# The state space model of the slice tokens, written anew: both directions on the two halves of the partitions, parameters loaded early, results kept transposed

## The chip, the cores and the metric

The kernel runs on one core of one Trainium2 chip. The metric is the device time of one execution in microseconds. A core has TensorE (PE in the profile; PEld are its weight loads), VectorE (DVE), ScalarE (ACT), GpSimd (POOL) and SyncE (SP). Each engine works through its own queue in order; DMA transfers run beside them. The granted clock is the share of its full clock that TensorE was given.

## The reference

A graph of 2708 nodes with 256 features goes through four layers, each an attention over the graph and a feed-forward block. The change lies in the feed-forward block of layer 0. There every node is softly assigned to 64 slice tokens in each of 8 heads, the tokens pass through a small state space model that runs both ways over the 64 tokens, and the result is handed back to the nodes:

```python
st = einsum('bhnc,bhng->bhgc', fx, sw) / (snorm + 1e-05)     # slice tokens: 64 tokens x 512
# _hydra(u = st):
zxbcdt = u @ in_w.T                 # gate z 512, x 512, B 64, C 64, dt 2*8
dt = softplus(concat(dt[..., :8], flip(dt[..., 8:])) + dt_bias)
xBC = silu(causal_conv(xBC, conv_w, 3 taps) + conv_b)
dA = exp(dt * -exp(A_log)); dBx = dt * B * x
h = h * dA_t + dBx_t; y_t = h . C_t                          # both directions
y = shift(y_fw) + shift(y_bw)
y = y + x * repeat(x @ fcD_w.T + Dp, 64)
yg = y * silu(z)
yg = yg * rsqrt(mean(yg**2) + 1e-05) * norm_w
ot = yg @ out_w.T
out = einsum('bhgc,bhng->bhnc', ot, sw) @ final_out_w.T      # back to the nodes
```

## The kernel before

All nodes lie in `X`, 22 tiles of 128 nodes by 256 features, float32. `cosine_gnn` is the graph attention of layer 0. `slice_ffn` follows. It allocates `swt` (the slice weights, transposed, of all nodes), `mix` and the output weights, then a pool `s_w` with the token sums `zs`, the weights `wfx`, `bfx`, `hyin` and `hyout` of the state space model, loaded through POOL's queue. The loop over the 22 node tiles computes logits, softmax and products; the sums of the tokens stay in four PSUM banks `zacc`. When the loop ends, DVE divides them into `zs` (lines 464 to 468), `hydra` runs, and a last loop of products (`po`, line 139 called from 477) adds `swt` times `mix` to `X`. Layer 1 begins from that `X`.

The order of each engine is chosen by a planner that places instructions as written, by priority, as soon as its model of the work says that they are ready; so work that is written earlier goes first where both are ready. `tc.issue_after` ties a block behind an instruction. `tc.manual_schedule(engines=...)` keeps the written order on the engines it names. In `slice_ffn` and `hydra` neither is used.

`hydra` turns the recurrence into matrices. For every head and direction, a 64x64 matrix of decays is the exponential of differences of cumulated sums, masked by a triangle, times B·C and the time step; both directions are shifted by one token and added into `km`. In order: transposes of `zs` into `zt` and `ztr` (L504, L508); the product with `wfx` and the bias, three products for each head (L139, L514), into `u`, 64 tokens on the partitions; four transposes of `u` to `ut` (L493); the gate `zg` with 512 columns at once and Silu (L523); the time step `dt`; the convolutions of x and of B and C (L543 to L554); x back to rows, `xr` (L561); softplus of `dt` by Exp and Ln (L567 to L581); the decays, two products for each head and direction (L615 to L619), each direction into its own bank of 64 partitions; on DVE and ACT min, Exp and three multiplications for each direction (L621 to L626); their sum in `km`; the product with `xr` (L650); the gate and the root mean square norm on rows (L651 to L660); transposes to `yt`; the product with `hyout` (32 passes, L139); and eight products with `outw` into `mix` (L671, L672). The PSUM pool `h_p` has three banks. Small parameters (`dtb`, `cw`, `cb`, `alog`, `fcd`, `dp`, `normw`) are loaded where they are used, through POOL's queue.

A float32 product appears in the profile as two passes of PE; a transpose as one.

Of the kernel before, what the change touches and what calls it, by code (L numbers as in the profile page):

```python
# [16 lines left out]
P = 128  # L17
# [375 lines left out]
def slice_ffn(net, wf, bf, early):  # L393
# [3 lines left out]
    with ExitStack() as ctx:  # L397
# [5 lines left out]
        with ExitStack() as c2:  # L403
            wp = c2.enter_context(tc.tile_pool(name="s_w", bufs=1))
            zs = wp.tile([P, 4, D + 1], F32, name="zs")
            wfx = net.load_weight(wp, a["w_fxT"], "wfx")
            bfx = wp.tile([1, HC], F32, name="bfx")
            nc.gpsimd.dma_start(bfx, a["b_fx"].partition_broadcast(1))
            hyin = net.load_weight(wp, a["hy_inT"], "hyin")
            hyout = net.load_weight(wp, a["hy_outT"], "hyout")  # L410
# [60 lines left out]
            hydra(net, wp, zs, wfx, bfx, hyin, hyout, outw, mix)  # L471
# [9 lines left out]
def hydra(net, wp, zs, wfx, bfx, hyin, hyout, outw, mix):  # L481


    nc, tc, a = net.nc, net.tc, net.a
    H, L, HC = 8, 64, 512
    ident = net.ident
    with tc.tile_pool(name="h_w", bufs=1) as w, tc.tile_pool(name="h_p", bufs=3, space=PSUM) as psum:

        def transposes(src, n, name):

            ps = psum.tile([P, n, L], F32, name="hp", tag="hp")
            for m in range(n):
                nc.tensor.transpose(ps[:, m, :], src[:, m * P : (m + 1) * P], ident[:L, :L])  # L493
            t = w.tile([P, n, L], F32, name=name)
            nc.scalar.copy(t, ps)
            return t


        zt = w.tile([P, 2, HC], F32, name="zt")
        ztr = w.tile([1, HC], F32, name="ztr")  # L500
        for c in range(2):
            ps = psum.tile([P, HC], F32, name="hp", tag="hp")
            for m in range(4):
                nc.tensor.transpose(ps[:, m * P : (m + 1) * P], zs[:, m, c * P : (c + 1) * P], ident)  # L504
            nc.scalar.copy(zt[:, c, :], ps)
        ps = psum.tile([1, HC], F32, name="hp", tag="hp")
        for m in range(4):
            nc.tensor.transpose(ps[:, m * P : (m + 1) * P], zs[:, m, D : D + 1], ident)  # L508
        nc.scalar.copy(ztr, ps)
        ps = psum.tile([L, HC], F32, name="hp", tag="hp")  # L510
        for h in range(H):
            hs = slice(h * L, (h + 1) * L)
            net.matmul_k(ps[:, hs], zt[:, :, hs], wfx[:, :, hs], last=False)
            nc.tensor.matmul(ps[:, hs], ztr[:, hs], bfx[:, hs], start=False, stop=True)  # L514
        u = w.tile([L, HC], F32, name="u")
        nc.scalar.copy(u, ps)
        ut = transposes(u, 4, "ut")


        pz = psum.tile([L, HC], F32, name="hp", tag="hp")  # L520
        net.matmul_k(pz, ut, hyin[:, :, 0:HC])
        zg = w.tile([L, HC], F32, name="zg")
        nc.scalar.activation(zg, pz, AF.Silu)  # L523
        pdt = psum.tile([L, 2, H], F32, name="hp", tag="hp")
        net.matmul_k(pdt.rearrange("p a h -> p (a h)"), ut, hyin[:, :, 1152:1168])
        dt = w.tile([L, 2, H], F32, name="dt")
        dtb = net.load_rows(w, a["dt_bias"], H, "dtb", L)
        nc.vector.tensor_tensor(dt, pdt, dtb.unsqueeze(1).to_broadcast([L, 2, H]), ALU.add)

        def conv(n, parts, offset, name):  # L530

            cw = w.tile([parts, n, 3], F32, name=f"cw{name}")
            nc.gpsimd.dma_start(
                cw, a["conv_w"][offset : offset + n * parts].rearrange("(n p) k -> p n k", p=parts)
            )
            cb = w.tile([parts, n], F32, name=f"cb{name}")
            nc.gpsimd.dma_start(cb, a["conv_b"][offset : offset + n * parts].rearrange("(n p) -> p n", p=parts))
            ps = psum.tile([parts, n, L], F32, name="hp", tag="hp")
            for m in range(n):
                o = HC + offset + m * parts  # L540
                net.matmul_k(ps[:, m, :], hyin[:, :, o : o + parts], ut)
            pad = w.tile([parts, n, L + 2], F32, name=f"pad{name}")
            nc.vector.memset(pad, 0.0)  # L543
            nc.scalar.copy(pad[:, :, 2:], ps)
            y = w.tile([parts, n, L], F32, name=f"y{name}")
            for m in range(n):
                nc.vector.tensor_scalar(
                    y[:, m, :], pad[:, m, 0:L], cw[:, m, 0:1], cb[:, m : m + 1], ALU.mult, ALU.add
                )
                for k in (1, 2):  # L550
                    nc.vector.scalar_tensor_tensor(
                        y[:, m, :], pad[:, m, k : k + L], cw[:, m, k : k + 1], y[:, m, :], ALU.mult, ALU.add
                    )
            nc.scalar.activation(y, y, AF.Silu)  # L554
            return y

        xt = conv(4, P, 0, "x")
        bc = conv(2, L, HC, "bc")
        ps = psum.tile([L, HC], F32, name="hp", tag="hp")
        for m in range(4):  # L560
            nc.tensor.transpose(ps[:, m * P : (m + 1) * P], xt[:, m, :], ident)  # L561
        xr = w.tile([L, HC], F32, name="xr")
        nc.scalar.copy(xr, ps)


        e = w.tile([L, 2, H], F32, name="e")
        nc.vector.scalar_tensor_tensor(e, dt, -1.0, dt, ALU.mult, ALU.max)  # L567
        nc.scalar.activation(e, e, AF.Exp, scale=-1.0)
        w1 = w.tile([L, 2, H], F32, name="w1")
        nc.vector.tensor_scalar(w1, e, 1.0, None, ALU.add)  # L570
        lg = w.tile([L, 2, H], F32, name="lg")
        nc.scalar.activation(lg, w1, AF.Ln)
        nc.vector.tensor_scalar(w1, w1, -1.0, None, ALU.add)
        same = w.tile([L, 2, H], F32, name="same")
        nc.vector.tensor_scalar(same, w1, 0.0, None, ALU.is_equal)
        nc.vector.tensor_tensor(w1, w1, same, ALU.add)
        nc.vector.reciprocal(w1, w1)
        nc.vector.tensor_tensor(lg, lg, w1, ALU.mult)
        nc.vector.tensor_tensor(lg, lg, same, ALU.add)
        nc.vector.tensor_tensor(lg, lg, e, ALU.mult)  # L580
        nc.vector.scalar_tensor_tensor(dt, dt, 0.0, lg, ALU.max, ALU.add)  # L581

        alog = net.load_rows(w, a["a_log"], H, "alog", L)
        nc.scalar.activation(alog, alog, AF.Exp)
        la = w.tile([L, 2, H], F32, name="la")
        nc.vector.scalar_tensor_tensor(
            la, dt, -1.0, alog.unsqueeze(1).to_broadcast([L, 2, H]), ALU.mult, ALU.mult
        )


        upper = w.tile([L, L], F32, name="upper")
        make_upper_triangular(nc, upper)
        strict = w.tile([L, L], F32, name="strict")
# [70 lines left out]
        for m in range(4):  # L664
            net.matmul_k(po[:, m, :], hyout[:, :, m * P : (m + 1) * P], yt)
# [1784 lines left out]
```

## Time and profile before

| | |
|---|---|
| median of 3 runs | 2646.69 us (2646.11 to 2649.6) |
| profiled execution | 2647.78 us |
| its span | 2646.0 us |
| mean granted clock | 0.962 |
| PE busy in the span | 2446.7 us (92%) |
| DVE, ACT, POOL busy | 1476.4 (56%), 1060.2 (40%), 329.2 us (12%) |
| slice loop, 410 to 500 us | PE 96% busy |
| state space model, 502.6 to 562.7 us | PE 74% busy, clock 0.63 |
| `po` loop, 562.7 to about 603 us | PE 97% busy or more |

Stages are given in microseconds from the start of the span. Busy shares of PE are of pipelined instructions whose ends are modelled: durations of single instructions overlap, and the distance from one start to the next is what a stream costs. The span is shorter than the execution by what lies around it, 1.8 us.

### The profile page before, as it was taken

Reading aid. Unit: us, or ns where it says so; the run is one execution under the profiler, and the core shown is the slowest. Engines: PE = TensorE matmul, PEld = TensorE weight load, DVE = VectorE, ACT = ScalarE, POOL = GpSimd, SP = SyncE. Lnnn points to the kernel's source line nnn. Section 1 sums busy time; section 2 is a strip of 40 time slices with the busy share of each in tenths; the row PEclk is TensorE's granted clock in tenths of the full one; section 3 lists DMA queues with packets and bytes.
Section 4 is the critical chain, followed back from the end, with each engine's and each line's share of the span. In section 5 each row is a group of like instructions: output and inputs, shape, how many; then the busy total and the mean of one; then the engine's idle time right before and its main releaser. Section 6 shows DMA issues by size and latency. Waiting matters only on the chain. (4 is left out here: it accounts for less than half of the span.)

```text
span 2646.0 us, 32568 instructions
## 1 busy us (share of the span) xinstructions
PE 2446.7 (92%) x11676; PEld 1581.2 (60%) x11676; DVE 1476.4 (56%) x3258; ACT 1060.2 (40%) x1714; POOL 329.2 (12%) x445
## 2 busy tenths in 40 slices
PE   5999999887999998979799989999899999969998
PEld 4666765574333334468578854444357777747887
DVE  7754348544788886333545457787653222264556
ACT  3444443313787772321434323334422222234454
POOL 1000002100000001134130011222231111110002
PEclk9999999978999999989899999999989999989999
DMA  8899520000000002774310010000231111050001
GB/s 289 281 299 320 172 86 31 3 6 1 1 1 1 1 1 82 170 193 144 91 62 1 1 38 9 19 17 17 101 128 50 33 33 33 22 203 7 1 1 43
DMA packets 106875, 197.70 MB, mean 75 GB/s; under 512 B 8846, under 2 KB 63736, under 8 KB 103876
## 3 DMA queue, kind: packets, MB, share of 16 engines
q1 hardware_dynamic: 88010, 146.82, 17.8%
q0 software_dynamic: 14896, 43.89, 5.1%
q10 hardware_dynamic: 3806, 4.85, 0.6%
q8 instruction: 98, 1.61, 0.3%
q14 instruction: 65, 0.53, 0.1%
HBM read 135.82 MB, written 59.71 MB: 74 GB/s over the span
## 5 line engine op out<-in xcount | busy, mean ns | idle before, releaser
L701 DVE SCALAR_TENSOR_TENSOR e<-e,mask 128x768 f32<-128x768 f32 (+3 forms) x352 | 417.0, 1215 | 241.9 <-ACT e L700 239.1
L700 ACT ACTIVATE e<-big_p,minus_one,ratio 128x768 f32<-128x768 f32 (+3 forms) x352 | 418.6, 1226 | 285.2 <-PE acc L1371 196.8
L1371 PE MATMUL acc<-V,e 128*128 128x257 f32 x1848 | 405.3, 382 | 5.7 <-DVE e L701 5.6
L1371 PEld LDWEIGHTS acc<-V,e 128*128 128x128 f32 x1848 | 352.7, 191 | 58.6 <-issue 7.0
L2125 PE MATMUL h<-w,ft 128*128 (+1 forms) x752 | 233.9, 452 | 1.3 <-DVE yl L1955 1.3
L307 PE MATMUL acc<-F,e 128*128 128x257 f32 (+1 forms) x924 | 212.5, 383 | 3.7 <-DVE e L303 3.4
L836 PE MATMUL acc<-e,V 128*64 128x512 f32 (+1 forms) x1056 | 209.1, 548 | 2.2 <-DVE e L701 2.2
L307 PEld LDWEIGHTS acc<-F,e 128*128 128x128 f32 (+1 forms) x924 | 171.6, 189 | 56.6 <-DVE e L303 29.2
L2142 DVE TENSOR_TENSOR hh<-hh,h 128x682 f32<-128x682 f32 x47 | 40.7, 865 | 243.7 <-PE h L2125 243.7
L2125 PEld LDWEIGHTS h<-w,ft 128*128 128x128 f32 x752 | 135.8, 191 | 57.2 <-issue 1.8
L836 PEld LDWEIGHTS acc<-e,V 128*64 128x64 f32 x1056 | 73.7, 138 | 151.3 <-issue 146.1
L1922 ACT ACTIVATE e<-sc 128x1024 f32<-128x1024 f32 (+4 forms) x131 | 107.1, 863 | 139.2 <-PE sc L1913 116.6
L303 DVE TENSOR_TENSOR e<-e,mask 128x512 f32<-128x512 f32 (+2 forms) x132 | 80.5, 621 | 141.3 <-ACT e L296 139.6
L1944 DVE TENSOR_TENSOR sum<-sum,e 128x1024 f32<-128x1024 f32 (+4 forms) x131 | 135.2, 1032 | 40.1 <-ACT e L1922 19.6
L296 ACT ACTIVATE e<-score 128x512 f32<-128x512 f32 (+2 forms) x132 | 69.4, 544 | 170.4 <-PE score L294 145.1
L2157 PE MATMUL po<-w,ht 114*128 (+1 forms) x564 | 131.5, 383 | 0.9 <-DVE ht L2150 0.9
L1913 PE MATMUL sc<-qt,kt 64*128 64x512 f32 (+5 forms) x568 | 123.9, 555 | 1.4 <-ACT sum L1922 0.9
L2157 PEld LDWEIGHTS po<-w,ht 114*128 114x128 f32 x564 | 107.6, 192 | 23.0 <-DVE ht L2150 8.2
L847 PE MATMUL den<-e,low 128*3 128x512 f32 (+1 forms) x1056 | 117.7, 542 | 0.0
L294 PE MATMUL score<-QK 128*128 128x512 f32 (+2 forms) x264 | 112.0, 553 | 3.4 <-ACT e L296 3.0
L1938 PE MATMUL po<-e,V 128*64 128x512 f32 (+5 forms) x524 | 111.2, 543 | 1.7 <-DVE e L1928 1.7
L2151 ACT COPY ht<-pt 114x256 f32<-114x256 f32 x47 | 17.5, 372 | 201.0 <-DVE ht L2150 201.0
(652 smaller groups left out, 3408.4 us busy)
## 6 DMA issues: line engine op xcount, KB each, us to landing
row<-in_adj SPq DMA_DIRECT2D x21, 1354.0 KB
raw<-in_adjT SPq DMA_DIRECT2D x35, 768.0 KB
hs<-zero SPq DMA_DIRECT2D x8, 2838.0 KB
hidden<-hr SPq DMA_DIRECT2D x32, 256.0 KB
wd<-in_f_wd SPq DMA_DIRECT2D x8, 1024.0 KB
kept<-mask SPq DMA_DIRECT2D x21, 338.5 KB
mask<-kept SPq DMA_DIRECT2D x21, 338.5 KB
w<-in_d_w1T SPq DMA_DIRECT2D x8, 682.0 KB
```

The costliest lines, as they stand in the source:

```text
L294: nc.tensor.matmul(ps[:r, :iw], QK[:, 0, span(j)], QK[:, 1, i0 : i0 + iw], start=True, stop=True)
L307: ended = nc.tensor.matmul(acc[k], e[:r, k * P : (k + 1) * P], F[:r, j, :], start=j == 0, stop=j == NT - 1)
L700: nc.scalar.activation(v, big_p[:, i], AF.Relu, bias=net.minus_one, scale=ratio)
L701: return nc.vector.scalar_tensor_tensor(v, v, 1.0, net.mask[:, j, i], ALU.add, ALU.mult)
L836: nc.tensor.matmul(acc[n][half, :iw], V[:, j, h, :], e[n][:, k, :iw], start=j == 0, stop=j == NT - 1)
L847: nc.tensor.matmul(den[g : g + Q, :iw], low[:, j, h, Q - 1 - q : 2 * Q - 1 - q], e[n][:, k, :iw], start=False, stop=j == NT - 1 and q == Q ...
L1371: nc.tensor.matmul(acc[k][:ri], e[:, k * P : k * P + ri], V[:, j, :], start=j == 0, stop=j == NT - 1)
L1913: nc.tensor.matmul(by_pairs(ps[:r, g], m, iw)[:, :, o:], kt[b, span(j)], qt[b, :, o:iw], start=True, stop=True)
L1938: nc.tensor.matmul(by_pairs(outs[n, p][b], m, iw)[:, :, o:], V[:r, j, g, :], by_pairs(e[:r, g], m, iw)[:, :, o:], start=j == 0, stop=j == ...
L1944: nc.vector.tensor_tensor(total, total, by_heads(e[:r], m, iw)[:, :, :, o:], ALU.add)
L2125: last = nc.tensor.matmul(halves[s, n][:, q, :HALF], fts[s][:, c, :], weights.w13[n][:, es[s], c, q * HALF : (q + 1) * HALF], start=c == 0 ...
L2157: last = nc.tensor.matmul(po, ht[:KP, k, :], w2[:KP, es[s], k, :], start=k == 0, stop=k == KC - 1)
```

## The change

`hydra` becomes a class. Its constructor stands where the weights were loaded, ahead of the slice loop, and now also loads all small parameters, takes the exponential of `a_log`, multiplies the rows of `hyout` by `norm_w`, clears the padding and `km`, and makes the triangles and a selector `pick`. `run` stands where `hydra` was called. It uses `manual_schedule` for PE, ACT and DVE, with seven PSUM banks.

- The product with `wfx` writes its result transposed, even heads on partitions 0 to 63 and odd heads on 64 to 127, so `u` and its transposes go.
- The forward direction lives on partitions 0 to 63 and the backward one on 64 to 127. Time step, softplus, min, Exp and the masks are done once for both. The half of the decays that doesn't depend on the row is one product of 512 columns for each direction. The sum over the directions is left to the product with `xr`, which holds x twice.
- The gate is computed transposed: 32 passes of 64 columns with full weight loads for 8 of 512 columns.
- y stays transposed: `yt` and its transposes go. The norm's factor is applied at the end, when `mix` is copied, on ACT and DVE in turn. The sum of squares is a product with ones.

```diff
-            wfx = net.load_weight(wp, a["w_fxT"], "wfx")
...
+            layer = Hydra(net, wp)
...
-            hydra(net, wp, zs, wfx, bfx, hyin, hyout, outw, mix)
+            layer.run(zs, outw, mix)
...
+    def __init__(self, net, pool):
+        self.wfx = net.load_weight(pool, a["w_fxT"], "wfx")
...
+        self.hyin = net.load_weight(pool, a["hy_inT"], "hyin")
+        self.hyout = net.load_weight(pool, a["hy_outT"], "hyout")
+        self.fcd = net.load_weight(pool, a["fcdT"], "fcd")
+        self.dtb = net.load_rows(pool, a["dt_bias"], H, "dtb")
+        self.alog = net.load_rows(pool, a["a_log"], H, "alog")
+        nc.scalar.activation(self.alog, self.alog, AF.Exp)
...
+        nc.gpsimd.dma_start(normw, a["norm_w"].rearrange("(c p) -> p c", p=P))
+        for c in range(4):
+            nc.vector.tensor_scalar(self.hyout[:, c, :], self.hyout[:, c, :], normw[:, c : c + 1], None, ALU.mult)
+        self.taps = {}
+        for name, n, parts, offset in (("bc", 2, L, HC), ("x", 4, P, 0)):
...
+            nc.gpsimd.memset(pad, 0.0)
+            self.taps[name] = n, parts, offset, cw, cb, pad
...
+        make_upper_triangular(nc, self.seen[low])
+        make_lower_triangular(nc, self.seen[high])
+        make_upper_triangular(nc, self.rise[low])
+        make_upper_triangular(nc, self.rise[high], val=-1.0, diag=False)
+        nc.vector.tensor_scalar(self.fall, self.rise, -1.0, None, ALU.mult)
+        self.pick = pool.tile([H, H, L], F32, name="pick")
+        nc.vector.tensor_copy(self.pick, net.ident[:H, :H].unsqueeze(2).to_broadcast([H, H, L]))
+        self.km = pool.tile([P, H, L], F32, name="km")
+        nc.gpsimd.memset(self.km, 0.0)
...
+            nc.vector.tensor_copy(ztr, pr)
+            nc.scalar.copy(zt[:, 0, :], pz[0])
+            nc.vector.tensor_copy(zt[:, 1, :], pz[1])
...
+                here = ps[halves[h % 2], h // 2, :]
+                nc.tensor.matmul(here, self.bfx[:, hs], ztr[:, hs], start=True, stop=False, skip_group_check=True)
+                for c in range(2):
+                    nc.tensor.matmul(
+                        here, self.wfx[:, c, hs], zt[:, c, hs], start=False, stop=c == 1, skip_group_check=True
+                    )
+            ut = w.tile([P, 4, L], F32, name="ut")
+            nc.scalar.copy(ut, ps)
...
+            front("bc")
+            front("x")
...
+            bc = convolved("bc")
+            nc.scalar.activation(bc, bc, AF.Silu)
+            pk = bank([P, H, L])
+            for b in halves:
+                nc.tensor.matmul(
+                    pk[b], self.fall[b], la[b].unsqueeze(2).to_broadcast([L, H, L]),
+                    start=True, stop=False, skip_group_check=True,
+                )
+            for h in range(H):
+                for b in halves:
+                    nc.tensor.matmul(
+                        pk[b, h, :], la[b, h : h + 1].to_broadcast([L, L]), self.rise[b],
+                        start=False, stop=True, skip_group_check=True,
+                    )
+            xt = convolved("x")
+            nc.scalar.activation(xt, xt, AF.Silu)
...
+            nc.vector.tensor_scalar(k, pk, 0.0, None, ALU.min)
+            nc.vector.tensor_tensor(gm, pg, self.seen, ALU.mult)
+            nc.scalar.activation(k, k, AF.Exp)
+            px = bank([P, HC])
+            for m in range(4):
+                for b in halves:
+                    nc.tensor.matmul(
+                        px[b, m * P : (m + 1) * P], xt[:, m, :], ident, start=True, stop=True, skip_group_check=True
+                    )
...
+            for m in range(4):
+                net.matmul_k(pz[:, m, :], hyin[:, :, m * P : (m + 1) * P], ut)
+            zg = w.tile([P, 4, L], F32, name="zg")
+            nc.scalar.activation(zg, pz, AF.Silu)
...
+                    pd[:, m, :], self.pick[:, 2 * m : 2 * m + 2, :].rearrange("h k l -> h (k l)"), fc,
...
+                    py[halves[h % 2], h // 2, :], xr[:, hs], km[:, h, :], start=True, stop=True, skip_group_check=True
...
+            nc.vector.tensor_tensor(y, py, through, ALU.add)
+            nc.vector.tensor_tensor(y, y, zg, ALU.mult)
+            sq = w.tile([P, 4, L], F32, name="sq")
+            nc.scalar.activation(sq, y, AF.Square)
+            po = bank([P, 4, L])
+            for m in range(4):
+                net.matmul_k(po[:, m, :], self.hyout[:, :, m * P : (m + 1) * P], y)
...
+            nc.scalar.activation(rs, ss, AF.Sqrt, bias=net.ln_eps, scale=1.0 / HC)
+            nc.vector.reciprocal(rs, rs)
+            ot = w.tile([P, 4, L], F32, name="ot")
+            nc.scalar.copy(ot, po)
+            for m in range(4):
+                pm = bank([P, D])
+                for b in halves:
+                    nc.tensor.matmul(pm[b], ot[b, m, :], outw[b, m, :], start=True, stop=True, skip_group_check=True)
+                if m % 2:
+                    nc.scalar.activation(mix[:, m, :], pm, AF.Copy, scale=rs)
                 else:
+                    nc.vector.tensor_scalar(mix[:, m, :], pm, rs, None, ALU.mult)
```

## The prediction

> **What bounds the kernel now.** I read the page, then a table of stages, then the groups by shape and the timeline of the state space model. The page's chain that ended last covers only the final 36 us, so this stage has to be read on its own. Stages first (stretch, length, busy PE, weight loads, DVE, ACT and POOL with counts, granted clock, DMA share, GB/s):
>
> ```profile
> 402.00:410.00 8.00, 5.64 (x20) 2.59 (x19) 7.56 (x18) 4.75 (x7) 3.29 (x5) 1.00 0.28 82
> 410.00:500.50 90.50, 86.72 (x363) 57.36 (x361) 75.35 (x138) 30.60 (x60) 19.18 (x38) 1.00 0.00 1
> 502.60:562.70 60.10, 44.32 (x275) 33.59 (x274) 19.85 (x65) 18.36 (x33) 8.26 (x18) 0.63 0.05 9
> ```
>
> The slice loop (410 to 500) is PE's, 96% busy. While it starts (402 to 410), DVE is the full engine. The state space model is 60.1 us of one chain: PE 74%, DVE 33%, ACT 31%, at a mean clock of 0.63. The same columns inside it:
>
> ```profile
> 506.00:508.00 2.00, 1.87 (x17) 1.40 (x18) 0.00 (x0) 0.37 (x1) 2.00 (x4) 1.00 0.21 5
> 508.00:510.00 2.00, 2.00 (x13) 1.53 (x14) 0.38 (x2) 0.00 (x0) 2.00 (x9) 0.50 0.10 2
> 516.00:518.00 2.00, 2.00 (x3) 0.47 (x3) 0.00 (x0) 0.12 (x1) 0.00 (x0) 0.50 0.00 0
> 518.00:520.00 2.00, 2.00 (x5) 0.55 (x4) 0.00 (x0) 0.00 (x0) 0.00 (x0) 0.94 0.00 0
> 528.00:530.00 2.00, 1.00 (x5) 0.55 (x5) 1.76 (x11) 1.14 (x3) 0.00 (x0) 0.62 0.00 0
> 552.00:554.00 2.00, 2.00 (x12) 2.00 (x11) 0.00 (x0) 0.00 (x0) 0.00 (x0) 0.50 0.00 0
> ```
>
> PE falls to half clock at 508, returns at 518 after the 512-column products of the gate (L139, hp<-hyin,ut), falls again at 528 and stays low to 566. At 552 PE is busy without a gap and still at 0.50: the 64-column stream with full weight loads doesn't lift the clock. Shapes (count, busy us, mean ns):
>
> ```profile
> L139 PE MATMUL hp<-yt,hyout 128*128 128x64 f32 x32 | 7.1, 423 | 0.5 <-ACT yt L495 0.5
> L139 PE MATMUL hp<-ut,hyin 128*128 128x64 f32 x32 | 3.8, 276 | 0.0
> L836 PE MATMUL acc<-e,V 128*64 128x512 f32 (+1 forms) x1056 | 209.1, 548 | 2.2 <-DVE e L701 2.2
> L294 PE MATMUL score<-QK 128*128 128x512 f32 (+2 forms) x264 | 112.0, 553 | 3.4 <-ACT e L296 3.0
> ```
>
> The first two are one shape at half and at full clock: 0.22 and 0.12 us each. The last two are 512 columns at full clock: 0.20 us each in L836, whose products alternate between two column halves of the array, 0.42 in L294, which has the whole array. So neighbouring halves overlap here. Last, the timeline at half clock (start, length):
>
> ```profile
> 530.44 0.44 PE L615 MATMUL hp<-upper,la 64*64 64x64 f32 x2
> ...
> 537.43 1.02 PE L139 MATMUL hp<-fcd,yx 128*64 128x8 f32 x8
> ...
> 562.73 7.50 PE L139 MATMUL po<-mix,swt 128*128 128x256 f32 x26 [0.46 <-ACT mix L672]
> ```
>
> 64 decay products, all in one quadrant, fill 530.44 to 537.43: 0.11 us each. The result is needed at 562.73.
>
> **The Trainium skill.** "TensorE: Matmul & The Clock Gate", Part 1, says PE runs at half clock by default, is released after a busy window of about 3.4 us, and loses it after an idle one. The trace agrees in the levels and, in 516 to 520, in the length; it adds that small products don't count as busy. Part 3 there says products in different row or column groups run at once; L836 agrees at 0.20 against 0.42. "TensorEngine Tiling (Array Packing)", Key Properties, says a change of tiling mode drains PE. "ScalarE: Activation LUTs", What ACT_TABLE_LOAD costs, has 1283 ns; the six loads here take 1.28 us each.
>
> **The change, in order**, on the clock of before and at half clock after 508.
>
> *Start.* The transposes end at 504.9 either way. The bias product now comes first and waits for `ztr`, which DVE copies ahead of the second half of `zt` (0.68 each, as L621's PSUM read): first head complete near 506.5, before 506.6. The products are the same 48, ending at 513.05. Gain 0.
>
> *Transposed results.* `u`, its four transposes and their copy go: 513.09 to 514.87 becomes one copy of 0.37 and a 0.06 hand-over, so PE resumes at 513.48. Gain 1.4.
>
> *PE from there*, counting two passes per product, 0.22 for a full load, 0.11 for a half load, and half of that where neighbours take different halves or quadrants: time step 16 at 0.055, 0.9; B and C 16 at 0.11, 1.8; x 32 at 0.22, 7.1; decays 4 of 512 columns at 0.85 (eight times 64 columns) in two quadrants, 1.7, and 32 at 0.055, 1.8 (before 7.0 for all); B times C 0.3; x as rows, 16 of 128 columns at 0.22 in two halves, 1.8; gate 32 at 0.22, 7.1; fcD 0.9; wait for `fc` 0.5; its spread over the heads, 8 at 0.22, 1.8; y 0.9; wait for DVE's two passes (0.3 to drain, twice 0.42 as 128x256, hand-overs) 1.2; output 32 at 0.22, 7.1; squares 0.9; root, `ot` copy and hand-overs 1.05; mix, 16 of 256 columns at 0.43 in two quadrants, 3.4 (seven banks, so no wait for a slot, where before three had PE wait for the copies); last copy 0.75. Sum 41.0: 513.5 + 41.0 = 554.5, against 562.73. Gain 8.2.
>
> *What lies under it.* Softplus and its table loads (513.5 to 519) hide under the x products, which end at 523.3. Then pad copy 0.6, twelve convolution passes 2.45 (as L547 and L551) and Silu 0.4 give x at 526.8, while the decays and B times C keep PE until 527.1: cover 0.3; without it each us is paid. The Silu of B and C stands behind the pad copy on ACT, which waits for PE at 523.3, plus 1.28 of table: ready 525.3, before PE asks at 526.8. The min, Exp and three kernel products on DVE (about 4 us) hide under the gate's 7.1. The Sqrt waits for the squares and `ot` is queued behind it, with all of mix behind that: that is the 0.9 and 0.3 in the sum. The deferred norm removes four 64x512 passes of DVE (0.68 to 0.74) and yt, about 4.7 us of the old chain, inside the 8.2. Memsets and triangles moved to POOL lay under PE before: 0.
>
> *Early loads.* Nine DMA issues of 0.53 to 0.78 move from 505 to 513 to about 390 to 396 on POOL, behind hyin and hyout; in front of outw and outb, which wait for space until 403 anyway. POOL's column of ones for the slice tokens shifts by some 9 us; its first use is after 405. New there: Exp of a_log on ACT (0.2) and four scalings of hyout on DVE, 128x512 each. Bounds 0.41 (the 64x504 copy) to 0.68; I take 0.55, so 2.2. They need the hyout and norm weights, whose queue drains near 401, so they fall where DVE is 95% busy and PE waits: paid in full. Cost 2.4.
>
> *Clock.* The decays and x rows are now dense over two quadrants or halves for 5.6 us, as dense as the gate products of before that lifted the clock. Released by about 528.7, the gate takes 3.8 instead of 7.1, and fcD, spread and y half: 5.1; a window that ends off that point costs about 1, so 4. Against it, the small steps before the output (fcD to y, about 4 us, mostly waiting) may drop it again. I take gained, then dropped.
>
> Sum: −8.2 − 4.0 + 2.4 = −9.8. The profiled execution took 2647.78 (span 2646.0, 1.8 around it), so 2638.0; the median of the runs is 1.1 lower, so 2636.9.
>
> **Rivals**, in the runs' median.
> A. Clock low throughout, as it was in 528 to 566: −8.2 + 2.4, 2640.9. For it: even a busy 552 to 554 stayed low. Against: dense pairs are another load.
> B. The forecast: 2636.9.
> C. The clock holds through the output: 3.3 there, 2.1 in squares and mix, and 1.6 in the first 3.3 us of po, which ran at half (562.7 to 566): 2629.9.
> D. Halves don't overlap for such short products: 0.9 (time step), 3.5 (decays), 1.8, 0.9, 0.9 come back, 8.0 in all, and no release: −0.2 + 2.4, 2648.9. L836 speaks against it, but with 512 columns.
> E. Slower: the scheduler places Exp of a_log or the first scaling where it thinks the load has landed, ahead of the graph stage's last exponentials or X updates. The load is behind 3.9 MB and tiny-element transfers; waited for from 392 to 406, ACT or DVE stands for up to 14 us, and with it the masks, X and the slice loop. −8.2 + 2.4 + 14 gives 2654.9. Past 5.8 us of stall there is no gain left under A. Before shows POOL waiting 3.4 us for outb in this place, so such waits happen.
>
> **Chances.** A 0.24, B 0.34, C 0.14, D 0.15, E 0.13. 0.2% is 5.3 us, about what a measurement of this kernel can tell from no change: faster means below 2641.4. A lies at the edge (0.18 of it faster), B and C are faster (0.47): 0.65. Same: the rest of A, D, short stalls: 0.23. Slower: long stalls and D with a stall: 0.12. The range for 8 in 10 runs from 2627 (C and a scaling that costs nothing) to 2649 (D); B's own is 2632 to 2640.
>
> **What would show it.** Right: PE resumes one copy after the last bias product; pairs of decay products start within 0.02 us; a granted clock of 1.00 in the gate products; the stage near 48 us; 2 to 3 us more between 400 and 410. Wrong: 64x64 products still 0.11 apart; clock 0.50 from 508 to the end; PE waiting for the Silu of x; a gap of several us on ACT or DVE that a load ended before 406; the graph stage after 604 put in another order.

## The result

The changed kernel takes 2641.03 us in the median of 17 runs (2630.93 to 2648.87), the kernel before 2648.32 us beside it (17 runs, 2643.68 to 2653.82). The ratio is 0.9973, with a 95% interval from 0.9962 to 0.9985: between 4.0 and 10.1 us faster, 7.3 by the medians. The profiled execution took 2634.70 us (span 2633.0, mean clock 0.966). It is one of the faster ones, so its 13 us against the profiled execution of before are not all the change's.

Stages of the changed kernel, the columns as in the prediction (stretch, length, busy PE, weight loads, DVE, ACT, POOL with counts, granted clock, DMA share, GB/s):

```profile
402.00:410.00 8.00, 5.02 (x9) 2.09 (x10) 3.38 (x11) 2.42 (x5) 6.76 (x18) 0.57 0.35 83
416.00:507.00 91.00, 87.56 (x371) 58.26 (x370) 76.28 (x142) 30.63 (x61) 17.54 (x36) 1.00 0.00 1
509.20:557.10 47.90, 42.20 (x310) 35.05 (x309) 15.19 (x53) 12.41 (x21) 1.81 (x3) 0.61 0.04 8
```

The slice loop itself is as it was. The state space model is 47.9 us long where it was 60.1, and PE is busy for 88% of it. But from 402 to 410, where DVE had 7.56 us of work, it now has 3.38, PE has about half as many instructions as before (9 for 20), and the granted clock, 1.00 before, is 0.57.

Inside the state space model, the timeline of PE of the changed kernel (start, length, instruction, idle time before it and what ended it):

```profile
533.04 1.97 PE L616 MATMUL hp<-la,fall 64*64 64x512 f32 x4
534.81 1.56 PE L622 MATMUL hp<-rise,la 64*64 64x64 f32 x30
...
537.63 3.79 PE L139 MATMUL hp<-ut,hyin 128*128 128x64 f32 x32
...
545.14 6.12 PE L139 MATMUL hp<-yh,hyout 128*128 128x64 f32 x32 [1.10 <-issue]
...
557.09 1.13 PE L139 MATMUL po<-mix,swt 128*128 128x256 f32 x4 [0.57 <-ACT mix L701]
```

The decays that filled 7 us are done in some 3.3 us (L616 and L622). The gate's 32 passes take 3.79 us, which is full clock; the output's 32 passes, of the same shape, 6.12, which is nearly all half clock. The clock records put the rise at 535.9 and the next fall at 546.2. `po` starts at full clock at once; before, its first 3.3 us ran at half.

**The ledger.** I paired each instruction that both programs hold and took the difference of its two start times. It is −0.5 us up to 380 us (nothing has changed there), +6.7 from 420 us to the end of the loop, −5.7 at the first `po`, −7.3 once `po` has caught up the half clock of before, and −13.0 at the end. So 7.2 us are lost between 380 and 410, 12.2 are gained from the last product of the loop to the first `po` (60.02 against 47.80 us), 1.6 in `po`, and 5.7 after that. In that last part both run the same instructions; what differs is the clock: the half-clock stretches after 570 us add up to 146.8 us before and 133.1 in the changed kernel's profile, and 13.7 us at half clock are worth up to 6.8. The first three terms make −6.6, close to the medians' −7.3. The prediction had −9.8.

### The profile page after: what moved, and what is told of

It reads as the page before. It is cut to its first block, busy times and chain, and to the rows that moved or that the text cites. A ratio compares the mean times of both kernels' runs of the same rounds, so it can differ in the third digit from the quotient of the medians.

```text
span 2633.0 us, 32640 instructions
## 1 busy us (share of the span) xinstructions
PE 2437.3 (93%) x11710; PEld 1579.9 (60%) x11710; DVE 1475.6 (56%) x3254; ACT 1053.4 (40%) x1703; POOL 330.9 (13%) x450
```

## The experiments

Each was compared with the kernel before on the same chip, in interleaved runs. The "jump" below is the shift of the loop (taken at 420 us) less the shift at 380 us. The "stage" runs from the end of the last product of the slice loop to the start of the first `po`: 60.0 us before, 47.8 in the changed kernel.

### Where do 7 us go before the loop?

Some names first: in the loop `f` is a tile of normalised nodes, `ft` its transpose, `pl` its logits and `sw` its slice weights; `e` and `g` are scores and sums of the graph layer ahead of the loop. `rise` and `fall` are triangles for the decays: POOL makes `rise`, and DVE makes `fall` from it.

The prediction had put 2.4 us there, for operations moved into a busy place. My first theory was just this with a larger size: the early operations hold up tile 0 in the queues. The rival was memory: the early tiles take 6.9 KB per partition (1 KB being 1000 bytes), which moves everything allocated after them. Two kernels undo the order, one makes the memory shift alone.

First, everything late:

```diff
+    def prepare(self):      # small loads, exponential, scaling, fills, triangles, pick
...
                 for t in range(NT + 2):
...
+                    if t == 6:
+                        layer.prepare()
```

> The changed kernel with everything of the state space model's constructor except the four weight loads (w_fx, b_fx, hy_in, hy_out) put into a method that the slice loop calls at tile 6: small loads, exponential of a_log, scaling of hy_out, zero fills, triangles, pick. The tiles keep their places in memory; the computation is the same. In the changed kernel the slice loop runs 6.7 us later than in the kernel before (the shift arises between 380 and 410 us). Theory O (the shift comes from these operations standing ahead of tile 0's work in the queues of DVE, ScalarE and GpSimd): the shift of the loop falls to under 1 us and the kernel to about 2635, some 6 us under the changed kernel. Rival M (the shift comes from the 6.7 KB per partition that the early tiles take, which moves the loop's work tiles onto memory that is freed later): the shift stays at 6 to 7 us and the time near 2641.

Measured: 2644.11 us, ratio 0.9982 (0.9972 to 0.9991). Jump 9.2 us.

Second, the loads stay and only the operations move:

> As the kernel above, but the nine small loads stay in the constructor and only the computing operations (exponential, scaling, fills, triangles, pick) move to tile 6 of the slice loop; the computation is the same. If the operations on DVE and ScalarE (pick ahead of tile 0's normalisation, scaling and exponential ahead of tile 0's logits) make the shift, it falls to under 1.5 us, time near 2635 to 2636. If GpSimd's queue of loads makes it (loads of 0.5 to 0.8 us of issue each, behind which the ones column of the first f tiles waits until 410 us), the shift stays at 5 to 7 us, time near 2641. Rival M also says 6 to 7 us.

Measured: 2642.25 us, ratio 0.9973 (0.9964 to 0.9983). Jump 8.4 us.

Third, the kernel before with a tile that nothing uses:

```diff
             hyout = net.load_weight(wp, a["hy_outT"], "hyout")
+            wp.tile([P, 1250], F32, name="unused")
```

> The kernel before with one unused tile of 5 KB per partition beside its weights (6.7 KB don't fit), so that the work tiles of the slice loop move in memory as in the changed kernel; nothing else differs and the computation is the same. Theory O: no shift in the slice loop, ratio 1.000 within 0.1 per cent. Rival M: the loop runs 5 to 7 us later, ratio 1.002 to 1.003.

Measured: 2655.27 us, ratio 1.0023 (1.0014 to 1.0032): slower than before, with no work more: the built program has the same instructions and two more waits. Jump 5.8 us.

The theory missed in all three runs, and the rival's cause is real. The first two runs don't acquit the operations, though. Written at tile 6, the scalings of `hyout` were still placed between 403.8 and 408.2 us, since the planner takes work that is ready; and in both, `fall` kept DVE waiting for POOL's triangle, for 3.36 and 2.50 us, after which PE stood for 2.89 and 2.68 us.

The profiles say how memory does it. In the kernel before, DVE has a pause at 399.5 us while it waits for the graph layer's last sums, and three tiles are normalised in it (timeline of DVE, kernel before):

```profile
399.50 1.03 DVE L124 TENSOR_SCALAR f<-X,mv,rstd 128x256 f32<-128x256 f32 x3
```

In the changed kernel the same pause stays empty, and the first `f` is written after the last work on the graph layer's tiles (timeline of DVE, changed kernel):

```profile
400.55 0.14 DVE L321 COPY den<-g 20x1 f32<-20x1 f32 x1 [1.44 <-ACT g L319]
...
401.68 0.47 DVE L327 SCALAR_TENSOR_TENSOR X<-F,s,X 20x256 f32<-20x256 f32 x1
...
402.53 0.39 DVE L124 TENSOR_SCALAR f<-X,mv,rstd 128x256 f32<-128x256 f32 x1
```

The unused tile does the same to the kernel before. Its timeline of PE:

```profile
403.64 0.66 PE L132 MATMUL tp<-ident,f 128*128 128x128 f32 x2 [2.96 <-DVE mv L161]
404.82 3.78 PE L139 MATMUL pl<-wf,ft 128*128 128x512 f32 x4 [0.52 <-ACT ft L429]
```

PE is starved for some 3 us, and then the logits take 3.78 us where they take 1.98 at full clock: the records show half clock for 6.8 us from 402.6. As the programs lay out their tiles, the pool of `f`, `ft` and `sw` ended 1.3 KB below the pool with the graph layer's last `e` and `g`. In the changed kernel it reaches 5.6 KB into that pool, in the third experiment 3.7 KB. Only the `sw` tiles and a few small ones lie in the shared part, but the pool waits as a whole. In the instruction streams of the changed kernel and of the third experiment, the first `f` carries a wait for TensorE's last product of the graph layer (L91) and stands behind DVE's last work on `X`; in the kernel before it has no such wait and stands 45 instructions earlier. And the third experiment shows that the unused tile alone does it.

So the next kernel brings the pools apart again, and leaves all early operations but the fills and the copy into `pick` early:

```diff
-        self.pick = pool.tile([H, H, L], F32, name="pick")
-        self.km = pool.tile([P, H, L], F32, name="km")
...
+            km = w.tile([P, H, L], F32, name="km")           # in run; the pads too
+            pick = w.tile([H, H, L], F32, name="pick")
```

> The changed kernel with the tiles pick and km and the padded convolution inputs (5.7 KB per partition) allocated, zeroed and filled in the state space model's own pool at its start in place of the constructor, so that the early tiles take 1.2 KB and the slice loop's work tiles end 0.1 KB below the first graph layer's work tiles (scores e and g), as they do in the kernel before (there 1.3 KB below). All loads, the exponential, the scaling, the fills of the triangles stay early; the computation is the same. Theory M (the loop's first tile waits because its pool reaches into memory of the graph layer's last scores): the jump of about 7 us between 380 and 410 us falls to 0 to 2.4 us (the scaling and the exponential that the prediction counted), and the time to 2634 to 2637. Rival O (the operations ahead in the queues): the jump stays at 5 to 7 us and the time near 2641.

Measured: 2637.26 us, ratio 0.9967 (0.9954 to 0.9980). Jump 5.9 us, so theory M, taken alone, missed as well. `f` of tile 0 is indeed early again (389 us), but PE now stops one tile later, for `f` of tile 1 (timeline of PE):

```profile
408.98 0.66 PE L132 MATMUL tp<-ident,f 128*128 128x128 f32 x2 [4.67 <-DVE f L124]
```

and DVE has four scalings of `hyout` in front of that `f` (timeline of DVE, same kernel):

```profile
406.60 1.84 DVE L499 TENSOR_SCALAR hyout<-hyout,normw 128x512 f32<-128x512 f32 x4
408.36 0.15 DVE L167 RECIPROCAL rstd<-sd 128x2 f32<-128x2 f32 x1
408.44 0.71 DVE L124 TENSOR_SCALAR f<-X,mv,rstd 128x256 f32<-128x256 f32 x2
```

With the operations early, the planner sets this `f` behind the softmax of tile 0 and the scalings; in the kernel before it went into the pause at 399.5. The scalings are only 1.84 of the 4.67 us, and ACT's wait of 1.56 us for `a_log` (404.36) comes before them too; what else holds this `f` was not separated.

Each cure alone leaves the other cause in place. Both together:

> The changed kernel with both cures of the early part together: the small loads and the early operations put to tile 6 of the slice loop, and pick, km and the padded inputs in the state space model's own pool, so that the loop's work tiles stay clear of the last graph layer's. The computation is the same. Each cure alone left the jump between 380 and 410 us at 6 to 9 us. Theory B (two causes, each of which alone holds the loop back: memory for the tiles' first writes, and the queues of DVE, ScalarE and GpSimd for the first tiles' further work; each is enough to starve TensorE once, which then runs at half clock for 6.8 us): with both gone the jump falls under 1.5 us, no half-clock stretch lies between 395 and 425 us, and the time is near 2635. Rival (something else, such as the weight loads or the planner's other order): the jump stays at 5 us or more and the time near 2640.

Measured: 2630.75 us, ratio 0.9938 (0.9925 to 0.9952). Jump 2.2 us. Its stage from 402 to 410 has the full clock again:

```profile
402.00:410.00 8.00, 4.60 (x14) 1.92 (x12) 7.67 (x15) 5.33 (x9) 6.45 (x10) 1.00 0.31 83
```

So there were two causes, each enough to starve PE for 3 to 5 us and to bring a half-clock stretch on top, and they overlapped instead of adding. One is the memory. The other is the early operations together with their small loads, which the last kernel moved at once and no run separates. The traces point to one operation that the prediction priced at nothing. In the changed kernel DVE stands until POOL has finished a triangle (timeline of DVE, changed kernel):

```profile
409.95 0.25 DVE L519 TENSOR_SCALAR fall<-rise 128x64 f32<-128x64 f32 x1 [4.28 <-POOL rise masks.py:66]
```

POOL makes its triangles after the small loads, and its queue stands until 402.81 us for the space of `outw`. Behind `fall`, in DVE's order, wait the `f` of two tiles (410.06 and 410.98 us) and the softmax of tile 0 (410.38). The length of this wait goes with the size of the jump. Five profiles have the changed kernel's early part: its own, and those of the four experiments below ahead of the combined ones. In two of them POOL spends 0.76 and 0.87 us on issuing the load of `outw`, `fall` waits 4.28 and 4.84 us, PE then stands for 2.13 and 2.26 us, and the jump is 7.2 us. In the other three the issue takes 2.45 us, `fall` waits 6.4 us, PE then stands for 3.15 us, a second stretch of half clock follows from 414 to 419 us, and the jump is 9.6 to 9.9. Why the same issue takes 0.8 or 2.45 us these runs don't say. No run removes this wait alone, so its part is read from the traces and not shown. In the kernel with room alone it isn't the whole: there `fall` waits 3.09 us, but only at 412.2, after PE's stop for `f`. In the kernel with both cures it doesn't wait at all.

The 2.2 us that remain there exceed the 1.5 expected; the scaling still lies at 405 to 410 us, though it is written at tile 6.

### The start of the stage

The transposes of `zs` used to run between the divisions; now they start after the last.

```diff
-            name="h_p", bufs=7, space=PSUM
+            name="h_p", bufs=4, space=PSUM
```

> The changed kernel with four PSUM banks in place of seven for the state space model; the computation is the same. Theory S (the first transposes wait for the last zs because the seven banks take in those of the z accumulators, which the zs instructions read): with four banks the transposes start by about 509 us in place of 510.85 and run between the zs instructions, and the stage from the end of zs to the first po is 1.6 to 2.2 us shorter (46.5 to about 44.5), unless one of the later steps then waits for a bank. Rival: the wait has another cause (order of the instructions), and the stage stays at 46.5 or grows.

Measured: 2637.89 us, ratio 0.9957 (0.9945 to 0.9968). The changed kernel, then this one (timeline of PE):

```profile
510.85 0.66 PE L546 MATMUL hp<-ident,zs 128*128 128x128 f32 x2 [1.57 <-DVE zs L464]
```

```profile
514.19 0.48 PE L546 MATMUL hp<-ident,zs 128*128 128x128 f32 x2
```

From the loop's last product to the first transpose it is −0.07 us in place of 1.57, and to the first product with `w_fx` and its bias 3.58 in place of 5.30 (2.76 in the kernel before). The whole stage is 46.8 us, only 1.0 shorter: the output ran nearly all at half clock (6.9 in place of 6.1 us), as the clock fell just when it began. No later step waits for a bank. Theory S is right: the wait was the reach of seven banks into those of `zacc`.

### Do neighbours on two halves overlap?

Taken away where the change has it:

```diff
-            for h in range(H):
-                for b in halves:
+            for b in halves:
+                for h in range(H):
                     nc.tensor.matmul(pk[b, h, :], ...
```

and likewise for `px`.

> The changed kernel with the loops of the decay products and of the x rows turned: all products of the lower half first, then all of the upper half, so that neighbours in TensorE's queue use the same quarter or the same column half; the computation is the same. Theory P (neighbours on different halves overlap): 16 decay products at 0.21 us each at half clock take 3.4 us in place of 1.56, the x rows 1.8 to 3.5 in place of 1.09: the stage from zs to the first po is 2.6 to 4.3 us longer; if the clock then isn't raised before the gate product, another 3.3 longer (gate 7.1 in place of 3.8). Rival: the products don't overlap and owe their time to the clock alone: both groups keep their times, no change of the stage beyond 0.5 us.

Measured: 2642.04 us, ratio 0.9988 (0.9981 to 0.9994). Stage 51.7 us, 3.9 longer. Groups of PE by shape (count, busy us, mean ns):

```profile
L622 PE MATMUL hp<-rise,la 64*64 64x64 f32 x32 | 3.3, 313 | 0.0
L639 PE MATMUL hp<-ident,yx 128*64 128x128 f32 x16 | 2.4, 378 | 0.0
```

They were 1.6 and 1.1, but that mixes two clocks: in the changed kernel the clock rose inside the decays, here only behind them. At the same half clock one pass of the decays starts every 0.106 us here, and two start every 0.107 us in the changed kernel. The clock was still raised before the gate (3.79 us), though later in the stage than in the changed kernel (30.65 us after the end of the loop in place of 26.65), so the release doesn't need these pairs. Nor did it come with the 512-column products, still paired here: they had ended 4.6 us before it.

Put in where the change doesn't have it, in the 24 products with `w_fx` and the bias, which go head by head and so use the same half three times running:

```diff
+            for h0 in range(0, H, 2):
+                for h in (h0, h0 + 1):
+                    nc.tensor.matmul(heres[h], self.bfx[:, hss[h]], ztr[:, hss[h]], ...)
+                for c in range(2):
+                    for h in (h0, h0 + 1):
+                        nc.tensor.matmul(heres[h], self.wfx[:, c, hss[h]], zt[:, c, hss[h]], ...)
```

> The changed kernel with the 24 products of w_fx and its bias put in another order: two neighbouring heads, whose results lie on the two column halves, take turns product by product (bias, bias, first chunk, first chunk, second, second); the computation is the same. If products on different column halves overlap as the decays did, the eight heads take 4 to 5 us at half clock in place of 8.2, and the denser stream may raise the clock earlier: stage 3 to 8 us shorter, time 2633 to 2638. Rival (the weight loads of 128 rows, 0.22 us each at half clock, set the pace and don't overlap): 8.2 us stay and the time near 2641.

Measured: 2631.42 us, ratio 0.9944 (0.9932 to 0.9957). Stage 44.6 us. The groups of the changed kernel, then of this one:

```profile
L558 PE MATMUL hp<-zt,wfx 128*64 128x64 f32 x32 | 5.5, 328 | 0.0
L556 PE MATMUL hp<-ztr,bfx 1*64 1x64 f32 x16 | 3.8, 337 | 0.9 <-DVE ztr L548 0.9
```

```profile
L562 PE MATMUL hp<-zt,wfx 128*64 128x64 f32 x32 | 2.8, 328 | 0.0
L557 PE MATMUL hp<-ztr,bfx 1*64 1x64 f32 x16 | 1.9, 337 | 0.9 <-DVE ztr L548 0.9
```

One instruction takes as long as it did (328 and 337 ns), but two run at a time: two heads in 1.03 us, where each took 1.02, at half clock. The weight loads of 128 rows overlap too, which the rival denied. "TensorEngine Tiling (Array Packing)", Key Properties, says so of loads and products on different tiles; here is its number. The clock rose no earlier for it, measured by the work: after the decays, where in the changed kernel it rose inside them. The products gained 4.1 us, of which the stage shows 3.2, as the output ran at half clock throughout (7.1 in place of 6.1 us).

### The clock at the end of the stage

Two products that nobody reads fill two of PE's waits:

```diff
+            fill = bank([P, HC])
+            nc.tensor.matmul(fill[:, :256], ident, xr[:, :256], start=True, stop=True)
             fc = w.tile([H, L], F32, name="fc")
...
+            nc.tensor.matmul(fill, ident, xr, start=True, stop=True)
             po = bank([P, 4, L])
```

> The changed kernel with two extra matrix products whose result nobody reads: one of 256 columns after the product with fcd (where TensorE waits 0.37 us for fc) and one of 512 columns after the product y (where TensorE waits 1.10 us for y on DVE); the result is the same. Theory C (the clock drops at 546 us because TensorE was thinly used in the 3.4 us before): the clock stays full through output and mix: output 3.8 in place of 6.1 us, squares 0.6 in place of 1.0, mix 1.9 in place of 3.7, less up to 0.8 for the extra products: the stage 3 to 4 us shorter, time near 2637. Rival (the output's own stream, half as dense as it could be, can't hold the clock): the clock drops as before and the extra products cost 0 to 0.8 us.

Measured: 2635.90 us, ratio 0.9953 (0.9940 to 0.9966). Timeline of PE:

```profile
544.82 3.76 PE L139 MATMUL hp<-yh,hyout 128*128 128x64 f32 x32
548.51 0.63 PE L691 MATMUL hp<-ones,sq 128*64 128x1 f32 x16
549.76 1.94 PE L702 MATMUL hp<-outw,ot 64*64 64x256 f32 x16 [0.62 <-ACT ot L698]
554.24 12.11 PE L139 MATMUL po<-mix,swt 128*128 128x256 f32 x55 [2.54 <-DVE mix L706]
```

Theory C holds: full clock through output and mix, 4.5 us less for the three groups. But the stage is only 2.6 us shorter (45.2), since PE then waits 2.54 us for the last `mix`. Why, is on DVE (timeline of DVE, same kernel):

```profile
550.46 0.48 DVE L706 TENSOR_SCALAR mix<-hp,rs 128x256 f32<-128x256 f32 x1 [0.82 <-PE hp L702]
553.28 0.42 DVE L717 TENSOR_TENSOR a1t<-w,av 128x256 f32<-128x256 f32 x1 [2.33 <-DMA av<-in_g_a]
553.62 0.48 DVE L706 TENSOR_SCALAR mix<-hp,rs 128x256 f32<-128x256 f32 x1
```

The next layer's first product stands between two copies of `mix` and waits for its load until 553.3. In the changed kernel the same product stood in the same place and waited until 555.70, and the second DVE copy followed at 556.04, when ScalarE's last copy (556.56) was still to come: the slower mix had been the cover of that wait.

### Together

> Both cures of the early part, four PSUM banks, and the w_fx products in turns on the two column halves, in one kernel; the computation is the same. If the gains add (6 early, 1.7 at the start, 4.1 in w_fx, less what the clock takes back): the first po starts near 546 us in place of 557, and the time is near 2629, ratio to the kernel before about 0.993. If theory B is wrong on the early part, the time is near 2635.

Measured: 2624.48 us, ratio 0.9913 (0.9900 to 0.9927). Jump 3.9 us (with one half-clock stretch at 413.8), stage 41.8 us, first `po` at 548.7 and not at 546.

To that, the two fills and

```diff
-                if m % 2:
-                    nc.scalar.activation(mix[:, m, :], pm, AF.Copy, scale=rs)
-                else:
-                    nc.vector.tensor_scalar(mix[:, m, :], pm, rs, None, ALU.mult)
+                nc.scalar.activation(mix[:, m, :], pm, AF.Copy, scale=rs)
```

> As the kernel above, with the two extra matrix products whose result nobody reads (they held the clock up through output and mix before) and with all four last copies of mix on ScalarE, so that none stands behind the next layer's product on DVE, which waited for a load (2.5 us before the first po in that run). The result is the same. Expected: output 3.8, mix 1.9 us, no wait of over 0.7 us before the first po: 4 to 5 us under the kernel above, time near 2625, ratio about 0.991. Rival: the clock, whose stretches change with each shift, takes it back: no more than 1 us under the kernel above.

Measured: 2622.21 us, ratio 0.9913 (0.9899 to 0.9927). Jump 1.6 us, stage 36.4. The end of its stage, timeline of PE:

```profile
537.56 1.94 PE L720 MATMUL hp<-outw,ot 64*64 64x256 f32 x16 [0.62 <-ACT ot L716]
540.08 20.12 PE L139 MATMUL po<-mix,swt 128*128 128x256 f32 x92 [0.57 <-ACT mix L721]
```

The wait is 0.57 again and the stage 5.4 us shorter. The time is less clear: by the medians it is 2.3 us less, by the ratio the same, so the gain is below the 4 to 5 us forecast. The rival's 1 us lies between these two figures, and the spread of the runs doesn't decide between them. The profiled executions can't either: they differ by 8.3 us, but the one of the kernel ahead is the slowest of its five runs (2627.68 us) and this one the fastest of its five (2619.36). Where the rest of the stage's gain goes stays open.

The last kernel ties the early block behind an exponential of the loop:

```diff
                     if t == 6:
-                        layer.prepare()
+                        with tc.issue_after(exp.ins):
+                            layer.prepare()
```

> The last kernel, with the block of small loads and early operations tied behind the exponential of tile 5 of the slice loop. Written at tile 6 and not tied, they had still been placed between 402 and 414 us, with 1.9 us of scaling among the first softmax steps, and the loop ran 1.6 us late. The result is the same. If that remainder is theirs, the jump between 380 and 410 us falls to 0 to 0.5 us, and the loop runs on undisturbed where they now lie: 1 to 2 us less than the kernel before it, median near 2621. Rival (the remainder is the planner's order of the first tiles): the jump stays near 1.6 us, median near 2622. What the clock does afterwards can hide a difference of this size in the time; the jump is what decides.

Measured: 2625.87 us, ratio 0.9910 (0.9894 to 0.9927), jump 1.6. It ran on another chip, where the kernel before took 2649.93 us beside it, so only the ratio compares. The stage is 39.6 us, as the mix ran at half clock, against 36.4. The tie moved ScalarE's exponential of `a_log` to 429.6 us and left DVE's scalings at 406.9 to 410.6. So the exponential isn't the remainder; whether the scaling is, wasn't decided.

All three are faster than the kernel before and than the changed kernel: their intervals end at 0.9927, the changed kernel's begins at 0.9962.

## Why the prediction was right, and where it was not

The forecast was 2636.9 us from −9.8; the medians give −7.3, in the range and faster. By the number alone rival A (−5.8) is the nearer one. The trace decides for B: the clock was raised before the gate, which took 3.79 us. The total misses because the early part costs 4.8 us more than was counted, while 1.6 us at the head of `po`, which weren't counted, give some back. The steps:

- *Start, gain 0: wrong.* It costs 2.5 us (2.76 to 5.30 from the last product of the loop to the first of `w_fx` or its bias). I had moved the bias product and its copy, and taken the transposes as unmoved. Seven banks move them behind the last `zs`, 1.7 us by the kernel with four banks. "So no wait for a slot" at mix was true and no gain: with four banks there was no wait either.
- *Transposed results, 1.4: right.* PE waits 0.46 us for `ut`, where 0.43 was counted.
- *PE from there: right, step by step.* Counted and measured, from start to start: time step 0.9 and 0.88 us, x with B and C 8.9 and 8.89, the 512-column decays 1.7 and 1.77; by length, squares 0.9 and 1.02, mix 3.4 and 3.68. That pairs overlap at 64 columns was taken from products of 512; the unpaired kernel shows it. So rival D is out. The 24 products of `w_fx` I priced as they stand, without asking whether they pair; 4.1 us lay there.
- *Clock, 4.0: right in kind.* Released at 535.9 us, before the gate (3.8 foreseen, 3.79 measured), dropped at 546.2, before most of the output, as chosen. The reason given, decays and x rows "as dense as the gate products of before", wasn't needed: the unpaired kernel's clock rose too. And "gained, then dropped" was taken without a working, so that part is luck. The stage as a whole gained 12.2 of the 8.2 + 4.0 = 12.2 foreseen, but the agreement is of errors that cancel, the start's 2.5 us being made up by what ran at full clock and was counted at half: x as rows (1.02 in place of 1.8), the tail of the decays (some 0.4), the first part of the output (6.1 in place of 7.1); the rest lies in the 1 us set aside for a release off the point. The 1.6 us at the head of `po`, which the prediction counted under C alone, came under B: the clock was back by 556.4.
- *Early loads, 2.4: the step that failed.* It is 7.2 us in the profile, and 9.6 to 9.9 in three others with the same early part. The reasoning was "they fall where DVE is 95% busy and PE waits: paid in full". In the changed kernel DVE is busy for only 3.38 of these 8 us. What is paid isn't the operations' length but engines that wait, and the half clock after a PE without work. One wait is for memory: moving it alone, with no operation, cost 5.8 us. The other, as the traces read, is `fall` for a good part: in the changed kernel it holds DVE for 4.28 us behind POOL, where the prediction had "Memsets and triangles moved to POOL lay under PE before: 0". The two runs meant to move the operations (9.2 and 8.4 us) hardly moved them, and `fall` still held DVE there. The prediction named the space that the outputs' weights wait for, and didn't ask where the new tiles push the loop's own.
- *Rival E, a stall of up to 14 us:* its mechanism appeared small. In the kernel with room, ACT waits 1.56 us for `a_log` ahead of its exponential.

What stays open: the 5.7 us after `po` has caught up, in the one profiled execution, of which 4.3 arise between 600 and 620 us, where the kernel before has half clock for 10.2 us and the changed kernel for 3.4; and the wider spread of the changed kernel's runs (18 us against 10). Both fit half-clock stretches that fall differently; no run here sets them.

## What to carry to other kernels

A tile allocated earlier moves all that is allocated after it: look at whose last reader the first writes of the next stage then have to wait for, in SBUF and in PSUM, before pricing the operations. An early operation that waits for another engine's queue holds up all that stands behind it in its own, however short it is. Order products so that neighbours in the queue take different halves, and price a starved PE together with the slow stretch that follows it. A step that gets faster uncovers what had waited behind it, here another layer's load in the same queue.

## What the runs showed of the hardware

- Two streams on the two column halves ran side by side even with 128-row weight loads and 64 columns: 2.8 us for 32 passes that took 5.5. A single row was no cheaper: in the changed kernel, at half clock, the two passes of a bias product start 0.16 us apart and 0.24 us before what follows, and of the four 128-row passes beside them the first two start 0.16 us apart and the last 0.24 us before what follows (0.11 between the others).
- About 1.8 us of unread products kept the clock up over the 9 us to the first `po`. "TensorE: Matmul & The Clock Gate", Part 1, ties the release to a busy window of about 3.4 us and the loss to an idle one. Here the window before the fall at 546.2, which takes in the output's first microsecond, was neither: PE was busy for 2.3 of its 3.4 us, with small products, and the clock fell. The output's own stream, without a gap, didn't raise it in 5.1 us at half clock (546.2 to 551.3) and didn't lose it in 3.76 us at full, in the run with the fills.
- After a gap of 2.96 us PE ran at half clock for 6.8 us, in the run with the unused tile; together they cost the loop 5.8 us. Kernels with the same early part met one such stretch or two.
- POOL's issue of one and the same load took from 0.76 to 2.45 us in kernels with the same early part.
